# Fixing the order of one feed-forward half's products in a fused transformer block, with four smaller moves

## The chip, the cores and the metric

The kernel runs on one core of a Trainium2 chip. A core has five engines that run side by side, each with its own queue of instructions: TensorE (PE in the profile: matrix products; PEld is its loading of weights), VectorE (DVE), ScalarE (ACT), GpSimd (POOL) and SyncE (SP), which here only issues DMA transfers. GpSimd issues some transfers too. Engines wait for each other through semaphores. The metric is the device time of one launch, in microseconds (us).

## The reference

A block of four residual steps on an input x of 2 × 1024 tokens by 512 features, in float32. `ln` is a layer norm without weights; all of it is computed in one launch.

```python
x = x + linear_attention(ln(x))   # 4 heads of 128, chunks of 128 tokens
x = x + ffn(ln(x))
x = x + softmax_attention(ln(x))  # one head of 512
x = x + ffn(ln(x))

# linear_attention, per chunk and head
k = k / max(norm(k), 1e-12)
alpha = sigmoid(x @ Walpha + balpha); beta = softplus(x @ Wbeta + bbeta)
cla = cumsum(log(alpha + 1e-6))
attn = (q @ k.T) * beta.T * where(causal, exp(cla - cla.T), 0)
y = attn @ v + (q @ state) * exp(cla)
state = state * exp(cla_end) + v.T @ (k * beta * exp(cla_end - cla))

# ffn: hidden size 1408, integer codes with a scale per row
W = (codes - 128) * scale[:, None]
ffn = (silu(x @ Wgate.T) * (x @ Wup.T)) @ Wdown.T
```

## The kernel before

**Split operands.** Matrix products run on float32 operands that are split into a high part, made by a ScalarE copy into the engine's shorter float format, and a low part, source minus high part, made by VectorE or GpSimd (`split`, L76 for the low part). A product is then two or three matmuls (`mm3`: high × high, high × low, low × high).

**Linear attention.** The loop at the heart of it runs over 16 tiles `t` of 128 tokens. One turn holds a quarter of a later group's query product (`q_head`), the next tile's key and value products (`kv_tile`), and `scores(t)`. That transposes the keys (`pkT`, copied to `kT`), computes the chunk's state (`pd` from `kw`, a GpSimd product of keys and a factor `s2`), calls `chunk_out(t-1)` (`pl` from `at`, `pg` from the state, result `xra` saved to `x1`), computes the scores `pS` and weighs them into `at`, with a factor `s1` and the decay `row`. The factor is made in `k_factor`: a sum of squares `ss`, a power −1/2 on GpSimd (L596), a product with beta on VectorE (L597). `gate_proj` computes the products `pc` of half of the values and the gates with the weights `wc`, once for each group of four tiles; `wc` is split on the way in (L76).

**What runs beside it.** The list `fill` spreads the steps of layer norms over the tiles: for a group of four tiles, four norm steps (statistics, `xn`, a block transpose on VectorE into `y`) and four moves, each of four DMA issues by SyncE (`xT` from `y`). From tile 12 on, `combine("f", 0)` makes the operands of the first feed-forward half, three steps at a tile: sums and differences of the quarters of `xT` (L252) and their splits `B11`, `T1`, `B22`, `T2`, `T3`, `B21`, `T4`. In the last tiles the product of `WvT` and `Wo` (`V0` to `V3`, results `pV`) is computed too, and the weights of the first feed-forward's first columns are prepared.

**Feed-forward.** `ffn` runs over two halves `pr` of the tokens. A half first goes over `j`, 11 groups of 128 hidden units. Gate and up products are one 2 × 2 block product by a scheme with seven products (P1 to P7, Winograd's form), so four result banks X, Y, Z, V and seven sums of weights and of tokens do what eight products would. For each `j`, `products` issues P1 into X, P6 into Y, P5 into Z and P7 into V, four matmuls each (L333); VectorE adds up u2, Z, V and `up`; and `finish` for `j-1` issues P2 into X, P3 into Z and P4 into V, then the activation and the product of gate and up (`sg`, `ha`, `hb`, splits `hs`). P2 reads `B21`, P3 `B22`, P4 `T4`, P5 `T1`, P6 `T2`, P7 `T3`. Then the half goes over 8 token tiles `i` with the second product (`pof`, L916 and L917). The sums of weights for a `j` are made by GpSimd in the first half (`stationary`, L316 to L319), saved to memory, and loaded again for the second half (L322): `wcf` in the first feed-forward, `wcg` in the second.

**What sets the order.** Instructions are written in the order above, but a scheduler with its own estimate of durations orders those of each engine by their dependences. The helper `behind(list)` adds an ordering: what is issued inside comes after the instructions in the list. PSUM has eight banks of 128 × 512; the pools of buffers in SBUF decide when a transfer into a reused buffer may start.

Of the kernel before, what the change touches and what calls it, by code (L numbers as in the profile page):

```python
# [13 lines left out]
ALU = mybir.AluOpType  # L14
AX = mybir.AxisListType

P = 128
# [17 lines left out]
def hybrid_block_kernel(ctx: ExitStack, tc: tile.TileContext, a, out):  # L35
# [11 lines left out]
    def psum(name):  # L47
        return pp.tile([P, 512], F32, tag="ps", name=name)
# [39 lines left out]
    def mm3(ps, lhs_hi, lhs_lo, rhs_hi, rhs_lo, first, last):  # L88
        nc.tensor.matmul(ps, lhs_hi, rhs_hi, start=first, stop=False)  # L89
        nc.tensor.matmul(ps, lhs_hi, rhs_lo, start=False, stop=False)  # L90
        end = nc.tensor.matmul(ps, lhs_lo, rhs_hi, start=False, stop=last).ins  # L91
        ends[id(ps)] = end
        return end
# [207 lines left out]
        codes(sp, "stg", c, a["wd"][j], f"cd{j}")  # L301
        nc.sync.dma_start(out=wd_d[j], in_=c)

    saves, held = [], {}

    def stationary(j, name, fresh=None, loaded=None, queue=None):


        w = slot(f"wc{name}_{j}").rearrange("p (n c) -> p n c", n=8)
        if fresh or loaded:  # L310
            a21, a11, s1, s2, s3, a12, s4, a22 = (w[:, n] for n in range(8))
            for n, (dst, nm) in enumerate(((w[:, 1:6:4], "cg"), (w[:, 0:8:7], "cu"))):
                room = (loaded[n], None) if loaded else fresh
                codes(*room, dst, a["wgu"][j][:, n * 512 : (n + 1) * 512], f"{nm}{name}_{j}")
            f = lambda x: x.bitcast(F32)
            nc.gpsimd.tensor_tensor(s1, f(a21), f(a22), ALU.add)  # L316
            nc.gpsimd.tensor_tensor(s2, f(s1), f(a11), ALU.subtract)
            nc.gpsimd.tensor_tensor(s3, f(a11), f(a21), ALU.subtract)
            nc.gpsimd.tensor_tensor(s4, f(a12), f(s2), ALU.subtract)  # L319
            saves.append(lambda: nc.sync.dma_start(out=wc_d[j], in_=f(w[:, 1:8])))  # L320
        else:
            (queue or nc.sync).dma_start(out=w[:, 1:8].bitcast(F32), in_=wc_d[j])  # L322
        return w

    def products(ps, w, nm, pr, n, first):
        m, x = {
            "P1": (1, "B11"), "P2": (5, "B21"), "P3": (6, "B22"), "P4": (7, "T4"),
            "P5": (2, "T1"), "P6": (3, "T2"), "P7": (4, "T3"),
        }[n]
        o = XT[nm, pr, x]  # L330
        for k in range(2):
            for s in range(2):
                nc.tensor.matmul(  # L333
                    ps,
                    w[:, m, k * P : (k + 1) * P],
                    o[:, s, k, :],
                    start=first and k == 0 and s == 0,
                    stop=k == 1 and s == 1,
                    skip_group_check=n != "P6",
                )  # L340


    with ExitStack() as actx:
# [76 lines left out]
        def gate_proj(st):  # L420

            if not vbs:
                vbs.append(slot("vb", F32).rearrange("p (n h d) -> p n h d", n=8, h=2))
            xh, xl = xTa[st]
            za[st] = z = sm([ST, 8], "z", st)
            for i in range(ST):
                cs = bass.ts(i, P)
                ps = psum(f"pc{st}_{i}")
                for k in range(KD):
                    mm3(  # L430
                        ps[:, 0:264],
                        xh[:, k, cs],
                        xl[:, k, cs],
                        wc[:, k, 0, 0:264],
                        wc[:, k, 1, 0:264],
                        k == 0,
                        k == KD - 1,
                    )
                vb = vbs[0][:, (st % 2) * ST + i].rearrange("p h d -> p (h d)")
                nc.vector.tensor_tensor(vb, ps[:, 0:256], bv_b[:, 256:512], ALU.add)  # L440
                nc.vector.tensor_tensor(z[:, i, :], ps[:, 256:264], bab_b, ALU.add)
# [145 lines left out]
        def k_factor(t, sq):  # L587
            st, i = divmod(t, ST)
            beta, ec, _ = sca[st]
            kf, v = kva[t]  # L590
            squared = normed[t][0]
            ss = mp.tile([P, H], F32, tag="ss", name=f"ss{t}")
            nc.vector.tensor_reduce(ss, sq, AX.X, ALU.add)
            nc.vector.tensor_scalar(ss, ss, 1e-24, None, ALU.max)
            s1 = mp.tile([P, H], F32, tag="s1", name=f"s1{t}")
            nc.gpsimd.tensor_tensor(s1, ss, mhalf.to_broadcast([P, H]), ALU.pow)  # L596
            scaled = nc.vector.tensor_tensor(s1, s1, beta[:, i, :], ALU.mult).ins  # L597
            normed[t] = squared, scaled
            kw = None
            if t % NC < NC - 1:  # L600
                s2 = mp.tile([P, H], F32, tag="s2", name=f"s2{t}")
                scaled = nc.vector.tensor_tensor(s2, s1, ec[:, 1, i, :], ALU.mult).ins
                kw = tl("kw", t)
                weighted = nc.gpsimd.tensor_tensor(kw, kf, s2.unsqueeze(2).to_broadcast([P, H, P]), ALU.mult)
                normed[t] = squared, scaled, weighted.ins
            kva[t] = kf, kw, v
            facta[t] = s1
# [116 lines left out]
        fill = [[] for _ in range(NT)]  # L724
        for src, nm, g, its in (
            (xa, "a", 2, (0, 0, 0, 1, 1, 1, 1, 1)),
            (xa, "a", 3, (2, 3, 4, 5, 5, 5, 6, 6)),
            (x1, "f", 0, (6, 6, 7, 7, 7, 7, 8, 8)),
            (x1, "f", 1, (9, 9, 10, 10, 10, 10, 11, 11)),
        ):  # L730
            for t, step in zip(its, ln_steps(src, nm, g)):
                fill[t].append(step)
# [8 lines left out]
        for t in range(NT):  # L741
            if t + 4 < NT:
                q_head(*divmod(t + 4, ST))
            if t == 0:
                decay_rows(0)
                load_row(0)
                load_row(1)
            load_row(t + 1)
            if t + 1 < NT:
                kv_tile(t + 1)  # L750
            weighed = scores(t)
            if t % ST == 0 and t + ST < NT:
                gate_proj(t // ST + 1)
            if t + 1 < NT:
                with behind((*(normed[t + 1][2:] or normed[t][2:]), *key_copy)):
                    decay(t + 1)
            if t == NT - 2:
                with behind(key_copy):
                    for n in (1, 2):
                        loads.append(product_operands(sp, a["WvT"], a["Wo"], "V", n))  # L760
                with behind(parts[-4:]):
                    late_norm.pop()()
            if t in (3, 7):
                with behind(key_copy):
                    a_split(t // 4 + 2)
            with behind(normed.get(t + 1, (weighed,))):
                for step in fill[t]:
                    step()
                if 1 <= t <= KH:
                    down_weights(sp, t - 1)  # L770
                for n in {NT - 3: (0,), NT - 1: (3,)}.get(t, ()):
                    loads.append(product_operands(sp, a["WvT"], a["Wo"], "V", n))
                if t == NT - 3:
                    first_codes = [
                        load_codes(xp, "xn", a["wgu"][0][:, n * 512 : (n + 1) * 512], f"cf0_{n}") for n in range(2)
                    ]
                if t == NT - 2:
                    wcs.append(stationary(0, "f0", loaded=first_codes))

                    room = staging("codes").bitcast(I32)  # L780
                    for j in (2, 3):
                        held[j] = [room[:, 2 * j - 4 + n] for n in range(2)]
                        for n in range(2):
                            nc.sync.dma_start(out=held[j][n], in_=a["wgu"][j][:, n * 512 : (n + 1) * 512])
                for n in range(3 if NT - 4 <= t < NT - 1 else 0):
                    moving.pop(0)()
                if t == NT - 1:
                    wcs.append(stationary(1, "f0", (sp, "stg")))
            if (t + 2) % ST:
                load_row(t + 2)  # L790
            if t == NT - 2:
                prep = weight_product(loads, "V")
            if t >= NT - 2:
                next(prep)
# [5 lines left out]
    def ffn(src, dst, nm, wcs, moving, ended, after):  # L800
# [3 lines left out]
        with ExitStack() as fctx:  # L804
# [5 lines left out]
            for pr in range(2):  # L810
# [90 lines left out]
                for i in range(2 * ST):  # L901
# [22 lines left out]
                    with behind(done):  # L924
                        for _ in range((0, 3, 3, 2, 2, 2, 2, 0)[i]):
                            if early or late:
                                (early or late).pop(0)()
                    if pr == 0 and i in (4, 6):
                        queue = None if i == 4 else nc.gpsimd
                        wcs += [stationary(n, f"{nm}1", queue=queue) for n in ((0, 1) if i == 4 else (2,))]  # L930

    of_b = combine("b", 0)
    ffn(
# [400 lines left out]
```

## Time and profile before

| | |
|---|---|
| Median of 3 runs | 933.04 us (932.44 to 934.39) |
| Profiled execution, its own time | 931.35 us |
| Span of the profiled execution | 929.6 us |
| TensorE busy | 920.4 us (99%), 4546 matmuls |
| VectorE busy | 724.9 us (78%) |
| ScalarE busy | 406.5 us (44%) |
| GpSimd busy | 217.0 us (23%) |
| Granted TensorE clock | 1.00 |

The profile comes from one execution. Its span runs from the first to the last instruction; 1.75 us of the execution's time lie outside it. The list of waits names for an engine's line the engine and line that released it, with the total, the number of times and the longest. A row of the timeline is an instruction or a run of equal ones: start, length, engine, line, operation, output and inputs, shapes, count, and in brackets the idle time before it with its releaser. Names are without numbers: `pXf` is X of the first feed-forward.

### The profile page before, as it was taken

The numbers are of one execution on the slowest core, as the hardware profiler recorded it, in microseconds if no ns is written. First come the engines' busy times: TensorE is split into PE (matmuls) and PEld (weight loads), VectorE is DVE, ScalarE is ACT, GpSimd is POOL, SyncE is SP. The second block draws the span as 40 slices with busy tenths as digits, with TensorE's granted clock in tenths as the row PEclk, the third lists the DMA queues.
The fourth block names the chain that finished last, engine by engine and source line by source line (L and its number), as shares of the span: only waits on it lengthen the run. The fifth ranks groups of instructions, "written<-read, shape, count | busy, mean of one in ns | idle before, by whom it ended". The sixth has DMA issues, their size and how long they took to land.

```text
span 929.6 us, 13541 instructions
## 1 busy us (share of the span) xinstructions
PE 920.4 (99%) x4546; PEld 778.7 (84%) x4546; DVE 724.9 (78%) x1485; ACT 406.5 (44%) x792; POOL 217.0 (23%) x320
## 2 busy tenths in 40 slices
PE   9999999999999999999999999999999999999998
PEld 8899998998788878888888888888888888888887
DVE  7876777779999789888948878559978876967654
ACT  5634344345665434444224545136434444444431
POOL 4233323444654002110120400040400530001100
PEclk9999999999999999999999999999999999999999
DMA  9535447685989366724742778315879742664022
GB/s 315 196 114 140 157 115 213 171 224 191 364 237 346 108 214 222 178 80 127 280 117 62 170 173 241 104 37 134 208 169 374 241 146 51 237 217 134 25 69 80
DMA packets 216182, 162.20 MB, mean 174 GB/s; under 512 B 151024, under 2 KB 167728, under 8 KB 216112
## 3 DMA queue, kind: packets, MB, share of 16 engines
q1 hardware_dynamic: 213200, 153.72, 54.9%
q0 software_dynamic: 2912, 7.61, 3.3%
q8 instruction: 36, 0.59, 0.3%
q14 instruction: 34, 0.28, 0.1%
HBM read 104.76 MB, written 41.84 MB: 158 GB/s over the span
## 4 chain that ended last, share of the span: by engine, by line
PE 89%; DMA 3%; DVE 3%; SPq 1%; POOL 1%; issue 1%; ACT 1%; POOLq 0%; DVEq 0%; ACTq 0%
PE pog L917 4%; PE pog L916 4%; PE pZg L333 4%; PE pVg L333 4%; PE pXg L333 4%; PE pXf L333 4%; PE pVf L333 4%; PE pZf L333 4%; PE pof L917 3%; PE pof L916 3%; PE pob L91 3%; PE pob L89 3%; PE pob L90 3%; PE psZ L1016 2%; PE psX L1016 2%; PE psV L1016 2%
## 5 line engine op out<-in xcount | busy, mean ns | idle before, releaser
L916 PE MATMUL pog<-wdg,hsg 128*128 128x512 f32 (+1 forms) x165 | 60.1, 375 | 0.0
L917 PE MATMUL pog<-wdg,hsg 128*128 128x512 f32 (+1 forms) x165 | 60.0, 375 | 0.0
L917 PE MATMUL pof<-wdf,hsf 128*128 128x512 f32 x154 | 59.1, 389 | 0.0
L916 PE MATMUL pof<-wdf,hsf 128*128 128x512 f32 x154 | 59.1, 389 | 0.0
L91 PE MATMUL pob<-vh,ptl 128*128 128x512 f32 x128 | 49.9, 390 | 0.0
L89 PE MATMUL pob<-vh,pth 128*128 128x512 f32 x128 | 49.9, 390 | 0.0
L90 PE MATMUL pob<-vl,pth 128*128 128x512 f32 x128 | 49.8, 389 | 0.0
L333 PE MATMUL pXf<-B_f,wcf 128*128 128x512 f32 x176 | 46.0, 392 | 2.3 <-DVE haf L844 1.3
L333 PE MATMUL pXg<-B_g,wcg 128*128 128x512 f32 x176 | 46.7, 389 | 0.0
L333 PE MATMUL pVg<-T_g,wcg 128*128 128x512 f32 x176 | 46.4, 389 | 0.0
L333 PE MATMUL pVf<-T_f,wcf 128*128 128x512 f32 x176 | 46.2, 390 | 0.0
L76 POOL TENSOR_TENSOR hsg<-sgg,hsg 128x128 fp32r<-128x128 f32 x40 | 18.0, 470 | 115.0 <-ACT hsg L75 79.0
L333 PEld LDWEIGHTS pXf<-B_f,wcf 128*128 128x128 f32 x176 | 32.7, 188 | 10.2 <-issue 2.0
L115 POOL TENSOR_TENSOR rs_g<-ve_g,mhalf 128x1 f32<-128x1 f32 x16 | 9.6, 605 | 132.3 <-DVE ve_g L113 132.3
L204 POOL DMA_DIRECT2D xT_g<-y_g x48 | 30.9, 651 | 39.2 <-DVE T_b L76 30.0
L115 POOL TENSOR_TENSOR rs_b<-ve_b,mhalf 128x1 f32<-128x1 f32 x16 | 10.4, 656 | 123.1 <-DVE ve_b L113 123.1
L333 PEld LDWEIGHTS pVf<-T_f,wcf 128*128 128x128 f32 x176 | 33.0, 188 | 7.1 <-DVE upf L873 0.3
L333 PEld LDWEIGHTS pXg<-B_g,wcg 128*128 128x128 f32 x176 | 33.0, 188 | 6.9
L333 PEld LDWEIGHTS pVg<-T_g,wcg 128*128 128x128 f32 x176 | 33.0, 188 | 6.9
L916 PEld LDWEIGHTS pog<-wdg,hsg 128*128 128x128 f32 x165 | 31.1, 188 | 5.6
L539 ACT ACTIVATE row<-row,ncl 128x128 f32<-128x128 f32 x64 | 20.4, 391 | 35.0 <-POOL row L528 34.9
L917 PEld LDWEIGHTS pog<-wdg,hsg 128*128 128x128 f32 x165 | 31.0, 188 | 5.6
(340 smaller groups left out, 2795.0 us busy)
## 6 DMA issues: line engine op xcount, KB each, us to landing
wcg<-wc SPq DMA_DIRECT2D x21, 896.0 KB, 5.4
wc<-wcf SPq DMA_DIRECT2D x11, 896.0 KB, 6.5
wcf<-wc SPq DMA_DIRECT2D x10, 896.0 KB, 6.2
p<-py SPq DMA_DIRECT2D x15, 512.0 KB, 3.3
ptl<-p SPq DMA_DIRECT2D x56, 128.0 KB, 3.2
xin_a<-in_x SPq DMA_DIRECT2D x16, 256.0 KB, 4.3
xra<-in_x SPq DMA_DIRECT2D x16, 256.0 KB, 3.6
row<-cl SPq DMA_DIRECT2D x16, 256.0 KB, 4.1
```

Of the source, the lines that this page charges most:

```text
L76: return c.ins, (eng or nc.vector).tensor_tensor(lo, src, hi.bitcast(F32), ALU.subtract).ins
L89: nc.tensor.matmul(ps, lhs_hi, rhs_hi, start=first, stop=False)
L90: nc.tensor.matmul(ps, lhs_hi, rhs_lo, start=False, stop=False)
L91: end = nc.tensor.matmul(ps, lhs_lo, rhs_hi, start=False, stop=last).ins
L115: nc.gpsimd.tensor_tensor(rs, ve, mhalf, ALU.pow)
L204: (nc.sync if sync else nc.gpsimd).dma_start(out=xf[32 * b : 32 * (b + 1), :, c, :], in_=y[32 * c : 32 * (c + 1), b].rearrange("p k i q -> ...
L333: nc.tensor.matmul(ps, w[:, m, k * P : (k + 1) * P], o[:, s, k, :], start=first and k == 0 and s == 0, stop=k == 1 and s == 1, skip_group_ ...
L539: nc.scalar.activation(row[:, h, :], row[:, h, :], AF.Exp, bias=ncl[:, n : n + 1], scale=-1.0)
L916: nc.tensor.matmul(ps, hs[i][0][:, j], wd[j][:, ds], start=j == 0, stop=False)
L917: nc.tensor.matmul(ps, hs[i][1][:, j], wd[j][:, ds], start=False, stop=j == KH - 1)
L1016: ends[nm] = nc.tensor.matmul(ps, o[:, i, k], w[:, j, k], start=first and k == 0 and i + j == 0, stop=k == 1 and i == 1, skip_group_check= ...
```

## The change

Five edits.

1. In the first half of the first feed-forward, the groups of four matmuls that `products` issues are put in the order in which they are written: each group comes behind the last matmul of the group before.
2. The factor `s1` of the last tile is multiplied by beta on GpSimd in place of VectorE. With it, the three steps of `combine("f", 0)` that stood in tile 14 (a difference in `xT_f1`, the splits `T2` and `T3`) move to tile 15, behind the weighing of its scores (`at15`).
3. In `gate_proj` the matmuls with the low parts of `wc` come after those with its high parts.
4. The norm steps and moves of the attention's token group 3 are spread over tiles 2 to 5, no longer 2 to 6.
5. The second half's first three weights are loaded at token tiles 3, 5 and 6, all through GpSimd's queue. Before, two were loaded at tile 4 through SyncE's and one at tile 6 through GpSimd's. This holds for both feed-forwards.

```diff
--- before.py
+++ after.py
@@ -301,7 +301,7 @@
         codes(sp, "stg", c, a["wd"][j], f"cd{j}")
         nc.sync.dma_start(out=wd_d[j], in_=c)
 
-    saves, held = [], {}
+    saves, held, ordered = [], {}, []
 
     def stationary(j, name, fresh=None, loaded=None, queue=None):
 
@@ -328,16 +328,18 @@
             "P5": (2, "T1"), "P6": (3, "T2"), "P7": (4, "T3"),
         }[n]
         o = XT[nm, pr, x]
-        for k in range(2):
-            for s in range(2):
-                nc.tensor.matmul(
-                    ps,
-                    w[:, m, k * P : (k + 1) * P],
-                    o[:, s, k, :],
-                    start=first and k == 0 and s == 0,
-                    stop=k == 1 and s == 1,
-                    skip_group_check=n != "P6",
-                )
+        with behind(ordered):
+            for k in range(2):
+                for s in range(2):
+                    end = nc.tensor.matmul(
+                        ps,
+                        w[:, m, k * P : (k + 1) * P],
+                        o[:, s, k, :],
+                        start=first and k == 0 and s == 0,
+                        stop=k == 1 and s == 1,
+                        skip_group_check=n != "P6",
+                    ).ins
+        ordered[:] = [end] if (nm, pr) == ("f", 0) else []
 
 
     with ExitStack() as actx:
@@ -426,16 +428,13 @@
             for i in range(ST):
                 cs = bass.ts(i, P)
                 ps = psum(f"pc{st}_{i}")
+                o = ps[:, 0:264]
                 for k in range(KD):
-                    mm3(
-                        ps[:, 0:264],
-                        xh[:, k, cs],
-                        xl[:, k, cs],
-                        wc[:, k, 0, 0:264],
-                        wc[:, k, 1, 0:264],
-                        k == 0,
-                        k == KD - 1,
-                    )
+                    w = wc[:, k, 0, 0:264]
+                    nc.tensor.matmul(o, xh[:, k, cs], w, start=k == 0, stop=False)
+                    nc.tensor.matmul(o, xl[:, k, cs], w, start=False, stop=False)
+                for k in range(KD):
+                    nc.tensor.matmul(o, xh[:, k, cs], wc[:, k, 1, 0:264], start=False, stop=k == KD - 1)
                 vb = vbs[0][:, (st % 2) * ST + i].rearrange("p h d -> p (h d)")
                 nc.vector.tensor_tensor(vb, ps[:, 0:256], bv_b[:, 256:512], ALU.add)
                 nc.vector.tensor_tensor(z[:, i, :], ps[:, 256:264], bab_b, ALU.add)
@@ -594,7 +593,8 @@
             nc.vector.tensor_scalar(ss, ss, 1e-24, None, ALU.max)
             s1 = mp.tile([P, H], F32, tag="s1", name=f"s1{t}")
             nc.gpsimd.tensor_tensor(s1, ss, mhalf.to_broadcast([P, H]), ALU.pow)
-            scaled = nc.vector.tensor_tensor(s1, s1, beta[:, i, :], ALU.mult).ins
+            eng = nc.gpsimd if t == NT - 1 else nc.vector
+            scaled = eng.tensor_tensor(s1, s1, beta[:, i, :], ALU.mult).ins
             normed[t] = squared, scaled
             kw = None
             if t % NC < NC - 1:
@@ -724,7 +724,7 @@
         fill = [[] for _ in range(NT)]
         for src, nm, g, its in (
             (xa, "a", 2, (0, 0, 0, 1, 1, 1, 1, 1)),
-            (xa, "a", 3, (2, 3, 4, 5, 5, 5, 6, 6)),
+            (xa, "a", 3, (2, 2, 3, 4, 4, 5, 5, 5)),
             (x1, "f", 0, (6, 6, 7, 7, 7, 7, 8, 8)),
             (x1, "f", 1, (9, 9, 10, 10, 10, 10, 11, 11)),
         ):
@@ -782,10 +782,14 @@
                         held[j] = [room[:, 2 * j - 4 + n] for n in range(2)]
                         for n in range(2):
                             nc.sync.dma_start(out=held[j][n], in_=a["wgu"][j][:, n * 512 : (n + 1) * 512])
-                for n in range(3 if NT - 4 <= t < NT - 1 else 0):
+                for n in range(3 if NT - 4 <= t < NT - 2 else 0):
                     moving.pop(0)()
                 if t == NT - 1:
                     wcs.append(stationary(1, "f0", (sp, "stg")))
+            if t == NT - 1:
+                with behind((weighed,)):
+                    for n in range(3):
+                        moving.pop(0)()
             if (t + 2) % ST:
                 load_row(t + 2)
             if t == NT - 2:
@@ -925,9 +929,8 @@
                         for _ in range((0, 3, 3, 2, 2, 2, 2, 0)[i]):
                             if early or late:
                                 (early or late).pop(0)()
-                    if pr == 0 and i in (4, 6):
-                        queue = None if i == 4 else nc.gpsimd
-                        wcs += [stationary(n, f"{nm}1", queue=queue) for n in ((0, 1) if i == 4 else (2,))]
+                    if pr == 0 and i in (3, 5, 6):
+                        wcs.append(stationary(len(wcs), f"{nm}1", queue=nc.gpsimd))
 
     of_b = combine("b", 0)
     ffn(
```

## The prediction

> **What bounds the kernel.** I read the page's engine shares first, then TensorE's list of waits, then the timeline of the stretches around each wait.
>
> ```profile
> span 929.6 us, 13541 instructions
> PE 920.4 (99%) x4546; PEld 778.7 (84%) x4546; DVE 724.9 (78%) x1485; ACT 406.5 (44%) x792; POOL 217.0 (23%) x320
> ```
> ```profile
> PE warm L677 <- POOL ones L351: 1.3, 1, 1.3
> PE pXf L333 <- DVE haf L844: 1.3, 1, 1.3
> PE pXf L333 <- DMA wcf<-wc: 1.1, 1, 1.1
> PE pl L660 <- DVE at L646: 0.8, 1, 0.8
> PE pd L627 <- POOL kw L604: 0.6, 1, 0.6
> PE pc L90 <- DVE wc L76: 0.3, 1, 0.3
> ```
>
> TensorE (PE) is busy for 99% of the span, and the change removes no matmul. So all that can be won is in the last five rows: 1.3 + 1.1 + 0.8 + 0.6 + 0.3 = 4.1 us. Beside its wait each costs a little more, which I read from the spacing of starts (in a run of 128x512 matmuls they follow each other at 0.227 us, 0.91 for a group of four). The whole is about 5.2 us, 0.56%. The average of 78% for VectorE (DVE) deceives at one place, the end of the attention and the first half of the first feed-forward:
>
> ```profile
> 200.00:225.00 25.00, 24.99 (x171) 22.68 (x170) 23.22 (x44) 12.56 (x27) 13.85 (x12) 1.00 0.75 246
> 225.00:250.00 25.00, 23.38 (x110) 18.98 (x108) 23.93 (x47) 17.15 (x27) 15.02 (x18) 1.00 0.78 294
> 250.00:275.00 25.00, 24.59 (x108) 20.25 (x109) 24.25 (x53) 14.99 (x29) 15.04 (x20) 1.00 0.85 274
> ```
>
> After the length of the stretch the columns are PE, weight loads, DVE, ScalarE (ACT), GpSimd (POOL). DVE has 23.9 of 25 us: here PE and DVE both bind, and the order in which PE asks for DVE's results decides. Two of the five waits lie here.
>
> **The change part by part.** The sum goes against the profiled execution (931.35 us, span 929.6, 1.75 around it), which is 1.69 under the median.
>
> Low parts of the gates' weights last: PE waits at 19 us for the last split of `wc` (0.3, and 0.28 of uneven spacing). With the low products last, 16 matmuls of 264 columns at 0.12 us (1.9 us) run first and cover it. −0.6; between 0 and −0.65.
>
> Norm steps of tile group a3 sooner: `pd8` waits for `kw8`, which waits for DVE, because at 138.38 DVE's `y_f` transposes stood 1.25 us for the moves of `xT_a`, and the backlog lasted to 152:
>
> ```profile
> 138.38 1.30 DVE L193 STREAM_TRANSPOSE y_f<-xn_f 128x512 f32<-128x512 f32 x2 [1.25 <-DMA xT_a<-y_a]
> ```
>
> With the moves one tile sooner, DVE is 1.25 earlier, `kw8` done at about 146.5, before PE's 147.2: −0.8 (0.71 + 0.1). What is late next is `kw4` at 97.7, which cost 0.19 and which an added `xn_a13` step passes by at another tile. Between 0 and −0.8.
>
> Last factor by GpSimd, three combine steps behind `at15`: now
>
> ```profile
> 223.39 1.02 POOL L596 TENSOR_TENSOR s<-ss,mhalf 128x4 f32<-128x4 f32 x1 [1.43 <-DVE ss L594]
> 224.44 0.16 DVE L597 TENSOR_TENSOR s<-s,beta 128x4 f32<-128x4 f32 x1 [0.50 <-POOL s L596]
> 224.52 1.22 DVE L252 TENSOR_TENSOR xT_f<-xT_f,xT_f 128x1024 f32<-128x1024 f32 x1
> 226.70 1.11 DVE L646 SCALAR_TENSOR_TENSOR at<-pS,s,row 128x128 f32<-128x128 f32 x4
> 227.09 0.49 PE L660 MATMUL pl<-sWv,at 128*128 128x128 f32 x2 [0.76 <-DVE at L646]
> ```
>
> A 128x4 multiply on POOL is not in the trace; the nearest rows are its 128x4 power (1.02) and its 128x1 power (0.56); DVE's own took 0.16. I take 0.5, nearest to the smaller operand. `at15` then starts at 224.97 instead of 226.70, as the 1.22 of `xT_f` no longer stands before it, and PE has four more matmuls of `pV` in front of `pl15` (226.17 to 227.08). The wait goes: −1.0. POOL's sums of `wcf0_0` fall behind the multiply, done about 229, needed at 231.7: nothing.
>
> First half's products in a fixed order (P1, P6, P5, P7 of j, then P2, P3, P4 of j−1). PE keeps its count of matmuls but may no longer run ahead. Now, from 239.2, PE does j=2's P1, P6, P5 then P3 of j=1 and P2 of j=2, before the low part of T4 is used, which DVE finishes at 244.46 (the second 243.25 row):
>
> ```profile
> 243.25 1.21 DVE L76 TENSOR_TENSOR T_f<-xT_f,T_f 128x1024 fp32r<-128x1024 f32 x1
> ```
> ```profile
> 246.49 2.65 PE L333 MATMUL pVf<-T_f,wcf 128*128 128x512 f32 x11
> 250.41 0.93 PE L333 MATMUL pXf<-B_f,wcf 128*128 128x512 f32 x3 [1.27 <-DVE haf L844]
> ```
>
> I walk both queues of the changed program with these durations, shifts of the earlier parts left out. PE from 226.17: 24 matmuls at 0.228 (`pV`'s, `pl15`, `pg15`, X0) to 231.65, then seven groups of 0.91 (Y0, Z0, V0, X1, Y1, Z1, V1) to 238.0. DVE steps 0.26 for 128x128, 0.60 for 128x512, 1.14 for 128x1024. `at15` 224.97 to 226.0, two `V` parts to 227.2, `xT_f` to 228.4; then it waits 1.0 for `pl15` on PE; `xra15` to 230.0, T2's low part 231.2, `xra15` 232.2, T3's low part 233.4, u2 234.0, four `V` results 236.4, two norm statistics 237.6, one sum 238.2, B21's low part 239.35. P2 of j=0 wants that at 238.3: 1.1 of wait. PE is then through P3 at 240.95. DVE: two sums and u2 of j=1 to 241.2, `xT_f` 242.4 (ACT's high part of T4 is there at 243.5), two sums, T4's low part 244.86. P4 of j=0 wants the high part at 240.95 and the low part right behind: 2.55 and 1.15 of wait. V of j=2 waits 0.3 for its u2. Together +5.1. The wait before X3 goes in return, since DVE does `haf` while PE still has four groups to do: −1.5 (1.43 and 0.08). After j=3 DVE has caught up; nothing else is late. Bounds for the +5.1: 3.0 if DVE's chain is 2 us shorter (below), 6.5 if it is longer.
>
> GpSimd and VectorE beside each other: in the trace two DVE casts of 128x1024 took 1.65 beside POOL's `row` selects, against 1.21 elsewhere, and the two `V2` parts 0.88 and 1.00 beside POOL's sums of `wcf0_0`, against 0.68. In the changed order these sums run at 225 to 228, beside the two `V3` parts and `xT_f`: +0.2 and +0.32 by the `V2` rows, up to +0.44 more if `xT_f` is met as those casts were, so +0.5 to +1.0 there, and −0.5 before `ss15`, where the `V2` parts run alone. I take zero, the `V2` rows on both sides, as the sums are about done when `xT_f` begins. [...]
>
> Second half's weights sooner: `wcf1_0` is issued at 334.96 by SP, behind saves, and lands 339.65; PE waits (1.22 + 0.11). From POOL's queue it is issued when PE has released its buffer, about 302, and the one such load in the trace took 7.7 us: landed about 310, needed at 338. −1.3. Behind the two loads on POOL, while the first waits for its buffer, stand only the third load (now at 318.76, after 25 us of idle time) and a norm step at 353.85, so nobody is held up; SP loses two issues of 0.4, on which nothing waits. In the second feed-forward PE has no such wait now: 0. The later `wcf1_8` load keeps its 0.13 us of slack, so 0 to +0.5.
>
> Sum: −0.6 −0.8 −1.0 +5.1 −1.5 −1.3 = −0.1: 931.2 for the profiled execution, 932.9 as a median.
>
> **The rivals.** (1) The early block is smaller. The chain to T4 is shorter if the GpSimd multiply takes DVE's 0.16 (−0.35), the `V2` parts run at 0.68 with nothing given back at `V3` (−0.5), and `pl15` is ready when DVE asks (−1.0). For it: each rests on one row, and all lie in one chain, so they add. Against: PE has `pg15` and a matmul of X0 to do before the last of `pl15`. Then the net is −2.0: 930.9. If DVE were done in time altogether, −5.2: 927.8.
>
> (2) Slower: VectorE, not PE, sets the stretch 205 to 245. DVE has 0.5 us of idle time between 206 and 224, so the 1.4 won before 150 would be spent waiting for it at `V1` and T4 (+1.4), and POOL's sums add their upper bound to the chain (+1.0): −0.1 + 2.4 = +2.3, 935.3. For it: 23.2 of 25 us busy. Against: what DVE does there is released by PE's own earlier matmuls (`state13`, `sq14`), so it moves with PE. It decides once DVE's chain moves by less than 1 us when PE comes 1.4 sooner.
>
> (3) The fixed order does nothing, if the scheduler had that order already: excluded, the rows from 239.23 show P2 of j=0 mixed with P1 of j=2, and P4 of j=0 after twelve matmuls of j=2.
>
> **How the numbers follow.** A measurement of this kernel can tell about 0.2% from no change, 1.87 us: faster is under 931.17, slower over 934.91. Forecast 0.48, its own range 931.0 to 935.0 (the bounds of 3.0 and 6.5 on the block): 0.06 faster, 0.36 the same, 0.06 slower. Rival 1 0.28: 0.24 faster, 0.04 the same. Rival 2 0.24: 0.22 slower, 0.02 the same. That is 0.30, 0.42 and 0.28. The range 929.6 to 936.0 goes to the middle of rival 1 (930.9 down to 927.8) and past rival 2's price by 0.7, for `kw` or the gates not gaining their 0.8 and 0.6; a tenth is left out on either side.
>
> **What would show it.** In the profile after, the waits for `wc`, `kw`, `at`, `haf` and the load of `wcf` are gone, and two rows are new: `pXf <- DVE B_f` of about 1.1 and `pVf` waiting for `T_f`, about 2.5 from ACT and 1.2 from DVE, at 237 to 245 us. PE's gaps between 225 and 252 sum to 5, not 2.5. If the new rows are under 2 in all, rival 1 holds; if the waits before 150 us are gone but V1 or T4 wait longer by as much, rival 2.

## The result: slower by 0.56%, and the profile after

The changed kernel took 938.86 us as a median of six runs (936.33 to 939.93), the kernel before 932.74 beside it (932.43 to 935.63): a ratio of 1.0056, 95% interval 1.0038 to 1.0073. That is 6 us above the forecast of 932.9 and outside the range. The profiled execution of the changed kernel is the quickest of its six, 936.33 us, with a mean granted clock of 0.998; the other five have 0.994 to 0.996.

The first lines of the page after, and TensorE's list of waits:

```profile
span 934.6 us, 13556 instructions
PE 922.1 (99%) x4546; PEld 778.7 (83%) x4546; DVE 725.5 (78%) x1484; ACT 406.6 (44%) x792; POOL 220.4 (24%) x325
```
```profile
PE pxT_a L125 <- DVE xn_a L117: 2.9, 2, 2.2
PE pVf L334 <- ACT T_f L75: 2.2, 1, 2.2
PE warm L677 <- POOL ones L353: 1.3, 1, 1.3
PE pXf L334 <- DVE B_f L76: 1.1, 1, 1.1
PE pVf L334 <- DVE T_f L76: 0.9, 1, 0.9
PE pd L627 <- POOL kw L604: 0.2, 1, 0.2
```

Of the five waits that the change could remove, those for `at`, `haf`, the load of `wcf` and `wc` are gone; of `pd`, the wait at 148 is gone and 0.2 is left, at 100 us. The rows `B_f` and the two of `T_f` are those that the prediction named, in the place and nearly the size that it gave. The first row was not foreseen. Of its 2.9 us, 0.75 lie at 15 us, in the start-up, where the profiles of the variants below have anything from 0 to 0.75. The other 2.2 lie at 40 us:

```profile
37.56 1.28 DVE L76 TENSOR_TENSOR Wv<-stg_Wv,Wv 128x256 fp32r<-128x256 f32 x2
38.76 0.94 DVE L117 TENSOR_SCALAR xn_a<-xin_a,mv_a,rs_a 128x512 f32<-128x512 f32 x1
```
```profile
39.76 0.65 PE L125 MATMUL pxT_a<-ident,xn_a 128*128 128x128 f32 x4 [2.18 <-DVE xn_a L117]
```

These are the timelines of DVE and PE after. `xn_a7`, the last norm that TensorE transposes ahead of `pWk0`, stands behind two splits of `Wv`. Before, it stood ahead of them and of two splits of the transposed norms (`xl_a`) and was done at 35.6, 2 us before it was needed (DVE's timeline before):

```profile
35.08 0.53 DVE L117 TENSOR_SCALAR xn_a<-xin_a,mv_a,rs_a 128x512 f32<-128x512 f32 x1
37.70 1.30 DVE L76 TENSOR_TENSOR Wv<-stg_Wv,Wv 128x256 fp32r<-128x256 f32 x2
```

The step itself also took 0.94 us instead of 0.53, beside GpSimd's own splits of `Wv` (37.60 to 39.42 in the trace after).

The second thing not foreseen stands behind the waits for T4, in PE's timeline after:

```profile
245.48 0.50 PE L334 MATMUL pVf<-T_f,wcf 128*128 128x512 f32 x1 [2.25 <-ACT T_f L75]
246.86 1.20 PE L334 MATMUL pVf<-T_f,wcf 128*128 128x512 f32 x3 [0.88 <-DVE T_f L76]
247.86 1.91 PE L334 MATMUL pXf<-B_f,wcf 128*128 128x512 f32 x4
249.56 1.67 PE L334 MATMUL pYf<-T_f,wcf 128*128 128x512 f32 x4
251.08 1.08 PE L334 MATMUL pZf<-T_f,wcf 128*128 128x512 f32 x4
```
```profile
247.60:251.00 3.40, 3.40 (x10) 2.64 (x9) 2.68 (x5) 1.20 (x3) 3.17 (x5) 0.53 1.00 350
```

Four matmuls that elsewhere take 1.07 take 1.91: starts 0.427 apart, not 0.227. The windows view gives the granted clock there, the column ahead of the DMA share, as 0.53 from 247.6 to 251, against 1.00 from 251 to 260. Eight matmuls at half rate cost 8 × 0.2 = 1.6 us. By the spacing of PE's starts, the three waits for B21 and T4 cost 4.8 us, the half rate 1.6 and the wait at 40 us 2.3, against 4.8 that the kernel before lost at `wc`, `kw`, `at`, `haf` and `wcf` and the changed kernel does not. That makes 3.9 of the 5.0 by which the spans differ; the rest is small pieces, the largest in the start-up.

### The profile page after: what moved, and what is told of

It is laid out like the page before. It is cut to its first block, busy times and chain, and to the rows that moved or that the text cites. A ratio compares the mean times of both kernels' runs of the same rounds, so it can differ in the third digit from the quotient of the medians.

```text
span 934.6 us, 13556 instructions
## 1 busy us (share of the span) xinstructions
PE 922.1 (99%) x4546; PEld 778.7 (83%) x4546; DVE 725.5 (78%) x1484; ACT 406.6 (44%) x792; POOL 220.4 (24%) x325
## 4 chain that ended last, share of the span: by engine, by line
PE 93%; DVE 3%; SPq 1%; DMA 1%; ACT 1%; issue 1%; POOL 1%; POOLq 0%; DVEq 0%
PE pog L921 4%; PE pog L920 4%; PE pof L920 4%; PE pVg L334 4%; PE pXg L334 4%; PE pZg L334 4%; PE pof L921 4%; PE pXf L334 4%; PE pVf L334 4%; PE pZf L334 4%; PE pob L91 3%; PE pob L89 3%; PE pob L90 3%; PE psZ L1019 2%; PE psV L1019 2%; PE psX L1019 2%
## 5 line engine op out<-in xcount | busy, mean ns | idle before, releaser
L334 PE MATMUL pXf<-B_f,wcf 128*128 128x512 f32 x176 | 48.3, 397 | 1.1 <-DVE B_f L76 1.1
```

The costliest lines, as they stand in the source:

```text
L334: end = nc.tensor.matmul(ps, w[:, m, k * P : (k + 1) * P], o[:, s, k, :], start=first and k == 0 and s == 0, stop=k == 1 and s == 1, skip_ ...
```

## The experiments

Each was timed beside the kernel before. The ratio is to that, with its 95% interval. Of an edit only the lines that bear on it are shown. X3 is the result bank X of `j` = 3, and so for the others.

**Without the fixed order (edits 2 to 5).**

```diff
-        ordered[:] = [end] if (nm, pr) == ("f", 0) else []
+        ordered[:] = []
```

> The changed kernel without the fixed order (edits 2 to 5 only). Theory: the fixed order costs its waits for B21 and T4 (4.8 us in the trace after) and eight matmuls at 0.427 instead of 0.227 us behind them (1.6), and gives back the 1.5 before X3; without it these go, the granted clock returns to 1.00, and only the new wait for xn_a at 40 us (2.3) stays against the gains of edits 4, 2 and 5 (0.8, 1.0, 1.3): 931 to 933 as a median, with the wait before X3 perhaps back. Rival (the loss is not from the order but from edit 2's moved combine steps): the waits for B_f and T_f stay and the time is over 936.

Measured: 936.16 us, ratio 1.0039 (1.0026 to 1.0053). The waits for B21 and T4 are gone, but the time stayed 3 us above the theory. Beside the wait at 40 us there is a new one, and half rate behind it again (PE's timeline):

```profile
260.91 2.04 PE L334 MATMUL pXf<-B_f,wcf 128*128 128x512 f32 x4 [2.67 <-DVE haf L848]
262.75 1.71 PE L334 MATMUL pYf<-T_f,wcf 128*128 128x512 f32 x4
```

So without the order X4 waits for `haf`, longer than X3 did before (1.3). The rival, that edit 2 brings the waits for B21 and T4, fell; but edit 2 was to turn out not innocent.

**With the gates' products in the old order (edits 1, 2, 4, 5).** The lines of edit 3 are put back.

> The changed kernel with the gates' products in the old order (edits 1, 2, 4, 5). Theory: the scheduler put xn_a7 behind two splits of Wv only because edit 3 changed the order around it; with the old order the wait of 2.3 us at 40 us is gone, the wait for wc of 0.5 at 19 us is back: 1.5 to 2.2 us less than the changed kernel, 936.7 to 937.4. Rival (the wait at 40 us is an accident of that execution's transfers): the same time as the changed kernel within 0.7.

Measured: 935.51 us, 1.0032 (1.0021 to 1.0043): 3.3 less than with edit 3, more than the 2.2 expected. The wait at 40 us is gone and that for `wc` back at 0.3. The rival fell: it is no accident of transfers.

**Edits 2, 4 and 5 alone.** Both of the above.

> Edits 2, 4 and 5 alone. Theory: the three gains stand by themselves (0.8, 1.0 and 1.3), neither new wait is there: 2.5 to 3.5 us under the kernel before, 929.3 to 930.3, clock 1.00. Rival (VectorE, not TensorE, sets the stretch 205 to 245 us): the gains of edits 4 and 2 are spent in a longer wait there and only edit 5's 1.3 is left: 931.5.

Measured: 932.1 us, 0.9990 (0.9979 to 1.0001). Neither theory nor rival fits: the waits for `kw` at 148 us, for `at15` and at 340 us went and none came at V1 or T4, yet in the profile PE lost 2.5 at X4, and eight matmuls ran at half rate (starts 0.40 to 0.43 apart, a granted clock of 0.57 from 258 to 262 us). (Seven of the eleven runs have a mean clock of 1.000, so the half rate is not in all of them.) The cause stands on DVE's timeline:

```profile
251.53 0.68 DVE L880 TENSOR_TENSOR upf<-pVf,upf 128x512 f32<-128x512 f32 x1
256.46 0.69 DVE L109 BATCH_NORM_STATS2 bn_f<-xin_f 128x6 f32<-128x512 f32 x1 [4.25 <-DMA xin_f<-x]
257.07 0.47 DVE L850 SCALAR_TENSOR_TENSOR sgf<-pVf,cols,sgf 128x256 f32<-128x256 f32 x1
257.46 0.48 DVE L851 SCALAR_TENSOR_TENSOR haf<-pVf,cols,sgf 128x256 f32<-128x256 f32 x1
```

DVE stands 4.25 us on `bn_f10`, the first step of a later tile's norm, which nobody needs yet, and `haf`, whose V bank PE wants, stands behind it. Before, DVE stood there 0.75:

```profile
253.94 0.69 DVE L109 BATCH_NORM_STATS2 bn_f<-xin_f 128x6 f32<-128x512 f32 x1 [0.75 <-DMA xin_f<-x]
```

**Zeros in the wait for T4.** All five edits, with 16 matmuls of zeros ahead of the first P4 group.

```diff
+        if n == "P4" and (nm, pr) == ("f", 0) and not zeroed:
+            zeroed.append(1)
+            with behind(ordered):
+                for _ in range(16):
+                    end = nc.tensor.matmul(ps, w[:, m, 0:P], nought.unsqueeze(1).to_broadcast([P, 8, 64]), start=False, stop=False, skip_group_check=True).ins
+            ordered[:] = [end]
```

> The changed kernel with 16 matmuls of zeros (512 columns, 3.6 us) put in front of the first P4 group, so that TensorE works through the wait for T4; they add zero and wait for nothing new. Theory: the half rate behind the wait comes from TensorE standing still; filled, the matmuls after it go at 0.227 and the granted clock is 1.00 although the first real P4 starts no sooner: 1.6 us less in the profile and 3 to 4 less in the median (the other executions of the changed kernel have mean clocks of 0.994 to 0.996 against the profiled 0.998), 934.5 to 936. Rival (the half rate has another cause, and the spread of the executions is that of transfers): as slow as the changed kernel, or slower by up to 0.5.

Here `nought` is a tile of zeros. Measured: 936.25 us, 1.0043 (1.0027 to 1.0059), just above the theory's range, clock 1.00 in the profile. PE's timeline:

```profile
243.26 3.93 PE L337 MATMUL pVf<-nought,wcf 128*128 128x512 f32 x16
247.03 1.07 PE L342 MATMUL pVf<-T_f,wcf 128*128 128x512 f32 x4
247.94 1.07 PE L342 MATMUL pXf<-B_f,wcf 128*128 128x512 f32 x4
```

The first real P4 product now starts at 247.03 instead of 245.48, yet X2 follows at 247.94, where it followed at 247.86 after, and runs at full rate: 1.07 us for its four matmuls, not 1.91, and a granted clock of 1.00 from 247.6 to 251, not 0.53. The median is 2.6 lower, though the two intervals overlap. What is shown directly is the rate: the half rate stands behind this wait in all three profiles in which PE stood still (after, edits 1, 2, 4 and 5, and the splits of `Wv` below), and not in this one. So the standing still makes it here, not the place.

**The fixed order alone on the kernel before (edit 1).**

> The kernel before with edit 1 alone. Theory: the fixed order brings its own waits for B21 and T4 whatever the other edits do: 3 to 5 us of waits at 238 to 247 us and half a dozen or more matmuls at half rate behind them, while the wait for at15 (0.8) stays and that before X3 (1.3) goes: 936 to 938.5. Rival (the order is harmless by itself, and only edit 2's later T2 and T3 make T4 late): at most 1 us of new waits, 932 to 933.

Measured: 935.03 us, 1.0022 (1.0011 to 1.0033). Waits of 1.6 and 1.4 for the two parts of T4, seven matmuls at half rate behind them (the four of `pXf` took 1.91 us), and the waits for `at15` (0.8) and `kw` (1.1) still there. The loss came out a little smaller than expected: B21 is in time here, and the wait for the load at 340 us, which no edit removes in this kernel, is not in its list either, as PE comes there later. T4 is late whatever edit 2 does.

**The gates' order alone on the kernel before (edit 3).**

> The kernel before with edit 3 alone. Theory: xn_a7 behind two splits of Wv, a new wait of 2.2 us at 39 us, half rate behind it in some executions; the wait for wc (0.3) goes: 934 to 936.5. Rival (it costs what the sum in the prediction says): 932.1, as the wait for wc is all that it touches.

Measured: 936.12 us, 1.0029 (1.0016 to 1.0041). The wait of 2.2 for `xn_a7` is there and that for `wc` is gone. Of the others, `kw` costs 1.1 instead of 0.6, and the load at 340 us none, as PE comes there later. Of its twelve runs six had a clock of 0.999 or 1.000, with a median of 934.8, and six 0.998, with 936.4, though single runs of the two groups overlap; of the 29 runs of the kernel before beside it one had 0.998. That would fit a stretch of half rate behind the 2.2 us wait in some executions. It is not shown: the profiled run has none, and where it lies in those six was not profiled.

**The splits of `Wv` behind `xn_a7`, all five edits.**

```diff
-        load_wv()
+        with behind(normed_x):
+            load_wv()
```

> The changed kernel with the splits of Wv ordered behind xn_a7, so that edit 3 stays and xn_a7 stands only behind the low part of a5. Theory: the wait at 40 us shrinks from 2.2 to about 0.7, and with it goes the half rate that some executions have there: 936 to 937. Rival (the extra 2.5 us of most executions over the profiled one comes from the waits at 241 to 248 us alone): 937.4, the 1.5 less and no more.

Measured: 937.07 us, 1.0046 (1.0028 to 1.0063). The wait shrank to 1.4, not 0.7, as `xn_a7` still stands behind two splits `xl_a` and takes 1.05 itself; the median fell by 1.8, though the intervals overlap. It does not tell the two theories apart.

**Edits 2, 4 and 5 with `bn_f10` behind `ha` of j=1.**

```diff
-                    with behind((sums,) if pr else ended if j < 3 else ()):
+                    with behind((sums,) if pr else ended if j < 3 else (kept[-2],) if (j, nm) == (3, "f") else ()):
```

Here `kept` lists the instructions that write `ha`.

> Edits 2, 4 and 5 with one norm step (bn_f10) ordered behind ha of j=1 on VectorE. In the profile of these three edits alone VectorE stands 4.25 us on bn_f10, whose input lands at 256.4, and ha, pZ and all of TensorE stand behind it (2.5 + 0.4 + 0.2 of waits and eight matmuls at half rate). Theory: in-order VectorE makes one late transfer into a wait of TensorE; with the step one place later these waits and the half rate go: 928 to 929.5, the three gains at last visible. Rival (VectorE has too much to do there, and whatever stands in front the wait comes back): within 0.7 of 932.1.

Measured: 930.44 us, 0.9978 (0.9969 to 0.9987). X4's wait and the half rate are gone (the profile's clock is 1.00), 1.7 less than without the line but short of the theory's 928 to 929.5; u2 of j=3, now the next behind `bn_f10`, makes PE wait 1.3.

**The same step behind the sums of j=3.**

```diff
-                    with behind((sums,) if pr else ended if j < 3 else ()):
+                    with behind((sums,) if pr or (j, nm) == (3, "f") else ended if j < 3 else ()):
```

> Edits 2, 4 and 5 with the norm steps of j=3 ordered behind the sums of j=3 on VectorE, four instructions later than in the run before, where u2 of j=3 still stood behind bn_f10 (a wait of 1.3 on TensorE at 259.6). Theory: bn_f10's input has landed when its turn comes, so the 1.3 and the 0.2 behind it go: 0.7 to 1.5 less than that run's 930.44, 929 to 929.7. Rival (VectorE's backlog): the wait moves to the next j, 930.4 again.

Measured: 929.2 us, 0.9956 (0.9941 to 0.9971), as expected and the fastest of all: 3.4 under the kernel before beside it. DVE does not stand on the step any more (its timeline; no idle time is marked):

```profile
258.27 0.68 DVE L880 TENSOR_TENSOR upf<-pVf,upf 128x512 f32<-128x512 f32 x1
258.87 0.68 DVE L109 BATCH_NORM_STATS2 bn_f<-xin_f 128x6 f32<-128x512 f32 x1
```

**Edits 4 and 5 alone.** The lines of edits 1, 2 and 3 are put back.

> Edits 4 and 5 alone. Theory: the waits for kw at 148 us (0.8) and for the load at 340 (1.3) go and nothing else moves: 930.2 to 931. The wait for at15 (0.8) and the one before X3 (1.3) stay. If so, edit 2 by itself is worth less than nothing (932.1 with it), as its later T2 and T3 put the norm step's wait in front of TensorE. Rival (edit 4 or 5 gives its gain back later): 932 or more.

Measured: 930.47 us, 0.9972 (0.9960 to 0.9983), in the range expected: the waits at 148 and 340 us are gone, and 2.1 us in the median, their sum in the prediction. But the theory's "nothing else moves" does not hold. PE's list still has the 0.6 for `kw` that the kernel before has, now at 98.6 us instead of 148:

```profile
PE pd L630 <- POOL kw L607: 0.6, 1, 0.6
```

So edit 2 cost 1.6 by itself (932.1; every run of the one is slower than every run of the other, though the intervals of the ratios overlap a little). With one norm step held back edits 2, 4 and 5 come out 1.3 under this (929.2), though there the intervals overlap. Holding the step back without edit 2 was not run, so how much of the 1.3 is edit 2's is open.

**The fixed order from j=3 on only (edits 1, 2, 4, 5).**

```diff
+        groups.append(n)
-        ordered[:] = [end] if (nm, pr) == ("f", 0) else []
+        ordered[:] = [end] if (nm, pr) == ("f", 0) and len(groups) >= 18 else []
```

> Edits 1, 2, 4 and 5 with the fixed order only from the products of j=3 on. Theory: the loss of the order lies in its first three j, where it asks for T4 and B21 before VectorE has them; without these no wait for T_f and B_f, clock near 1.00, 931 to 932.5, about the time of edits 2, 4 and 5 alone (932.1), with the wait for bn_f10 still there in some form. Rival (the order costs over the whole half): over 934.

Measured: 934.15 us, 1.0015 (1.0004 to 1.0025), just over the rival's 934. The B21 wait is gone, T4's is down to 0.3 and the profile's clock is 1.00, so the first three j do carry a part of the loss. But of the 3.4 us that the whole order costs over edits 2, 4 and 5, 2 stay: PE waits 1.6 and 1.1 for `haf` and three times, 1.4 together, for `sgf` of ScalarE in front of a V product. A fixed order takes every late bank in turn.

## Why the prediction was wrong

The range reached 936.0, and the block's bound of 6.5 us covered the fixed order. Edit 3 went past the bounds given for it, and edit 2, for which none were given, went the wrong way. In medians the way from before to after can be walked: edits 4 and 5 give −2.1 (930.47), edit 2 takes +1.6 (932.1), edit 1 +3.4 (935.51), edit 3 +3.35 (938.86). The prediction had −2.1, −1.0, +3.6 and −0.6. The steps depend on their order: on the kernel before, edit 1 alone costs 2.4 and edit 3 alone 3.5.

*Edit 3, the step that failed.* "With the low products last, 16 matmuls … run first and cover it. −0.6; between 0 and −0.65." The cover is real and the wait for `wc` did go. But the sum looked at PE's order alone. The scheduler also reordered VectorE's queue in that stage, and `xn_a7` went behind the splits of `Wv`: 2.3 us of PE's time in every profile with edit 3 unmended. In half of the runs of that edit alone the clock is lower as well, with 1.6 more. It is the largest miss, 4.0 us in the median, and the upper bound of 0 was wrong: an edit that moves a schedule has no safe sign. Of the 4.0 the wait explains 2.3. For the rest, the mean clock of the runs falls from 0.997 without edit 3 to 0.9955 with it, about 1.4 us by the estimate in the last section; where that lies was not traced.

*Edit 2, the other one.* Its wait is gone, with the multiply on GpSimd at 0.20 us instead of the 0.5 taken, and no wait at V1 or T4 took its place: −1.0 as said. That it costs 1.6 in all was missed, 2.6 us, at the sentence "After j=3 DVE has caught up; nothing else is late". In the profile of edits 2, 4 and 5 `xin_f10`, the input of `bn_f10`, was issued by SyncE at 250.95, where before it was 248.14 (248.25 with edits 4 and 5 alone). It landed 2.5 us later than before, and DVE came to it 1 us earlier. The prediction followed VectorE's queue only as far as T4, and not SyncE's. Why SyncE's queue is later there was not tried.

*Edit 1.* The walk of the two queues held: 1.1, 2.55 and 1.15 were worked out, 1.06, 2.25 and 0.88 measured, and X3 no longer waits. Its total of +3.6 is near the +3.4 measured, but by two errors that cancel. The sum took matmuls at 0.227 us on both sides of the wait, and eight ran at 0.427, twelve in the profile of edits 1, 2, 4 and 5. In return the order takes away more than X3's wait, because PE comes to X4 later: in the full change DVE stood 3.0 us on `bn_f10` and PE did not wait for it, where without the order it lost 2.5. On the kernel before, without edit 2, the order cost 2.4 (935.03), with the wait at 340 us (1.1) hidden behind it.

*Edits 4 and 5* came out as summed, but in part by luck. The wait for the load (1.3) is gone. That for `kw8` is gone too, but `kw4`, which the sum let pass because an added step would pass it by, cost 0.25 in the profile after and 0.16 to 0.87 in the other nine with edit 4, 0.59 with edits 4 and 5 alone. There PE reaches the first `pV` product at 214.43 us, in the kernel before at 214.40, so edit 4 had won 0.2 us at most by then (that execution's start-up was that much longer). The 0.8 fits the median's sum and is not in the profile.

*The rivals.* None of them is what happened. Rival 2's direction was right, but its mechanism did not show: PE's lists have no wait at V1. Nor was it put to the test, as the 1.4 us before 150 was won in no profile: PE reached the first `pV` product 0.4 us sooner than before with edits 2, 4 and 5, and 1.8 later with the full change. Rival 1's shorter chain to T4 did not come, although GpSimd's multiply was nearly as short as it asked: the high part was awaited for 2.25.

## What to carry to other kernels

Where a scheduler orders the queues, read the order of every engine near the edit, not only of the one that is edited: here a reordering of PE's products cost 2.3 us through a norm step on VectorE. On a queue that runs in order, a step that nobody needs yet must not stand in front of one that TensorE waits for, unless its input is sure to have landed; moving one such step was worth 3 us with edit 2 in place, more than edits 4 and 5 together. A wait that is taken away can come back at the next one like it, as `kw8`'s did at `kw4`. And a fixed order pays only where every operand is early: it swaps the waits that the profile shows for all those that the scheduler had been stepping round.

## What the runs showed of the hardware

The granted clock fell to half (0.50 from 247.42 to 250.82 us in the profile after) behind waits that the prediction priced at their length alone. In the profiles PE ran eight matmuls at half rate after one wait of 2.48 us (edits 2, 4 and 5) and six after one of 2.67 (without the fixed order); eight after waits of 2.25 and 0.88 with one matmul between (the full change), and twelve in two other profiles with the same two waits; seven after 1.62 and 1.41 (edit 1 alone). After single waits of 1.3 to 1.6 it ran on at full rate (1.27 in the kernel before, with a granted clock of 1.00 from 250.3 to 254), and after the 2.2 at 40 us it did so in all four profiles that have it (1.00 from 40 to 44 in the profile after).

By the granted clock the stretch of half rate was 3.4 us long in the profile after, and 6.8 us in the two profiles with twelve matmuls, whose mean clock was 0.996; by the spacing of starts it cost 1.5 to 2.7 us. The fall came at 247.42, 0.56 us behind the end of the second wait (246.86) and not with it. One stretch of 3.4 us lowers the mean clock of a launch by 0.0018, half of 3.4 over 934.6. So, as an estimate, the clocks of 0.998, 0.996 and 0.994 in the runs of the changed kernel stand for one, two and three stretches, which fits its spread from 936.33 to 939.93. Where the further ones lie was not profiled.

By these runs a wait like the one of 2.48 us is to be priced with a stretch of half rate as a risk on top, and so are two close together like those of 1.62 and 1.41. Whether one of 2.2 brings it in some executions was not shown.
